# Two TensorE allowances in an order account, and two more adds of exp by DMA, in a fused attention and expert kernel

## The chip, the cores and the metric

The kernel runs on one core of a Trainium2 chip. The metric is the device time of one execution in microseconds (us), as a median over several executions. Almost all executions of one build lie within 0.3% of its median, the widest within 0.4%. Every profiled run of this study was of the fast state. A ratio is the mean time of one kernel's fast runs over the mean of the other's fast runs of the same rounds, so it is not quite the ratio of the medians that are quoted beside it. All verdicts use ratios to the kernel before; 0.01 is 35 us.

PE is TensorE's matmul, PEld its weight load, DVE VectorE, ACT ScalarE, POOL GpSimd, SP SyncE. "Attention" is here the time from the first exp of layer 0's attention to the last, "the tail" the time from there to the start of the experts' gated products, "experts" the rest.

## The reference, cut to what matters

The input is 8 images of 256 channels and 32 x 32 points, all in fp32.

```python
# layer 0: 8 heads of 32 channels; keys and values are the maps pooled by 1, 2, 3 and 6 and convolved
attn = softmax(einsum('bhqd,bhkd->bhqk', q_g, k) * SCALE)      # q: 1024 points, k: NK pooled points
out_att = einsum('bhqk,bhkd->bhqd', attn, v)
...                                                            # mixing by a global token, projection
x = x + layer0(groupnorm(x))
# layer 1 on the tokens of each image, then 8 experts with soft gates
t = t + attention(layernorm(t))                                # x @ Wq, Wk, Wv, softmax over 1024 tokens
t = t + experts(layernorm(t))
```

## The kernel before: the parts that matter here

The kernel is one program whose order is made while it is built. The main loop walks through the 384 steps of layer 0's attention (8 images, 2 groups of four heads, 2 halves of the points, 12 chunks of keys). Everything else, layer 1 too, is a thread of small pieces, which an "order account" slips in between.

```python
for i in range(len(steps) + 1):
    ...
        pts[i] = scores(b, c, sl, kc)          # 4 tiled matmuls into sc (one buffer), exp by ScalarE into pt
        f.step()                               # threads of the other engines may go ahead
    ...
        values(b1, c1, kc1, pts[i - 1], pv)    # 4 tiled matmuls from pt
        if kc1 % 2:                            # odd chunk: added to the even one, by DMA
            add(kc1, pts.pop(i - 1), pts[i - 2])
            pairs.append(pts.pop(i - 2))
    ...
        f.step(PACE)                           # threads may now use PACE us of TensorE

def scores(b, c, sl, kc):
    ...
    pt = T(work, [P, 4, 512], "pt", bufs=6)    # six buffers of 1 MB for exp
    f.act.activation(pt[:w], t[:w], AF.Exp, scale=SCALE0)

def add(kc, pt, into):                         # accumulating DMA, issued by GpSimd
    f.pool.dma_start(out=into..., in_=pt..., accum_op=ALU.add)

def sums(n, pairs):                            # the sum of exp of one unit (12 steps, 6 pairs)
    for i in range(1, NKC // 2):
        yield until(lambda: len(pairs) > i)
        for j in range(0, 4, 2):               # pairs 1 to 5 onto pair 0, by VectorE
            s = pairs[0][:, j : j + 2, :]
            yield ve(s, pairs[i])
            f.ve.tensor_tensor(s, s, pairs[i][:, j : j + 2, :], ALU.add)
```

The account holds an estimated clock for each engine. A thread's next matmul is put in if its data would be there in time, and if the thread's use of TensorE in this step is within the allowance `PACE` (or TensorE would wait for the exp anyway):

```python
def runnable(self, need):
    ...
        return (not self.closed and (self.credit > 0 or pe < until - 0.5)
                and at + MARGIN <= until and slot <= until)

def resume(self, thread):
    pe = self.now["PE"]
    thread[1] = next(thread[0], None)
    ...
    self.credit -= self.now["PE"] - pe
```

The account also assumes a landing time for DMAs that GpSimd issues, `LANDING = 9.5` us. It decides only which pieces are taken to be ready; the hardware waits for the real landing.

## Time and profile before

| | before |
|---|---|
| time, median of 3 (6 with later rounds) | 3497.31 us (3496.12) |
| profiled execution's span | 3505.2 us |
| attention / tail / experts | 1993.9 / 304.3 / 1100.2 us |
| PE idle in attention / tail | 191 / 27.0 us |
| ScalarE's wait for a pt buffer held by a DMA add | 56.9 us in 17 waits |
| DMA engines' busy share in attention | 0.54 to 0.56 |

PE is the busiest engine in every stage, so an engine's idle time counts only where PE in turn waits for that engine. "PE sc <- ACT pt" is such a line: the scores have one buffer, and PE may not overwrite it until exp has read it. If exp itself stands in front of a pt buffer that a DMA still reads, PE's wait is a DMA's doing although the line names ScalarE. The lines themselves are in the prediction.

### The profile page before, as it was taken

The numbers are of one execution on the slowest core, as the hardware profiler recorded it, in microseconds if no ns is written. First come the engines' busy times: TensorE is split into PE (matmuls) and PEld (weight loads), VectorE is DVE, ScalarE is ACT, GpSimd is POOL, SyncE is SP. The second block draws the span as 40 slices with busy tenths as digits, with TensorE's granted clock in tenths as the row PEclk, the third lists the DMA queues.
The fourth block names the chain that finished last, engine by engine and source line by source line (L and its number), as shares of the span: only waits on it lengthen the run. The fifth ranks groups of instructions, "written<-read, shape, count | busy, mean of one in ns | idle before, by whom it ended". The sixth has DMA issues, their size and how long they took to land.

```text
span 3505.2 us, 39918 instructions
## 1 busy us (share of the span) xinstructions
PE 3237.3 (92%) x15276; PEld 1790.8 (51%) x15276; DVE 2278.6 (65%) x3922; ACT 1676.3 (48%) x2195; POOL 489.1 (14%) x616
## 2 busy tenths in 40 slices
PE   7787899899989989989999997998999999999998
PEld 3322244344424434433544354745777777777776
DVE  6686888778878787685554443314776656666665
ACT  3565766556566565555564542332223333333332
POOL 2122122131131221321121110004000000000000
PEclk9798999999999999999999999999999999999999
DMA  1356655645655564554555556223440000000000
GB/s 47 75 107 152 134 127 111 144 108 111 148 105 110 134 136 109 119 124 111 112 125 136 128 105 219 79 79 107 150 150 19 19 18 24 31 18 19 19 12 20
DMA packets 103880, 333.28 MB, mean 95 GB/s; under 512 B 12848, under 2 KB 38200, under 8 KB 80448
## 3 DMA queue, kind: packets, MB, share of 16 engines
q0 software_dynamic: 24576, 172.51, 25.1%
q1 hardware_dynamic: 75744, 156.16, 13.0%
q8 instruction: 122, 2.00, 0.2%
q10 hardware_dynamic: 3360, 1.97, 0.2%
q14 instruction: 78, 0.64, 0.1%
HBM read 96.23 MB, written 61.87 MB: 45 GB/s over the span
## 4 chain that ended last, share of the span: by engine, by line
PE 53%; DMA 3%; DVE 3%; ACT 2%; issue 1%; POOL 0%; SPq 0%; DVEq 0%; ACTq 0%; POOLq 0%
PE bank L667 24%; PE y L667 11%; PE sm L667 9%; PE sc L667 3%; PE sx L667 3%; PE pv L667 3%; ACT pt L667 2%; DMA pt<-pt 1%; DMA t<-xr 1%; DVE acc L667 1%; DVE rec L667 1%; DMA t<-t 0%; DMA hn<-hn 0%; DMA xr<-in_x_dram 0%; DVE t L667 0%
## 5 line engine op out<-in xcount | busy, mean ns | idle before, releaser
L667 ACT ACTIVATE pt<-sc 128x2048 f32<-128x2048 f32 (+1 forms) x384 | 720.5, 1876 | 358.5 <-PE sc L667 263.0
L667 PE MATMUL sc<-q,kn 32*128 32x512 f32 (+1 forms) x3072 | 460.8, 671 | 134.1 <-ACT pt L667 132.7
L667 DVE SCALAR_TENSOR_TENSOR acc<-p,vec,acc 128x225 f32<-128x225 f32 (+7 forms) x928 | 521.1, 568 | 34.0 <-ACT acc L667 9.3
L667 PE MATMUL bank<-h,w2e 128*128 128x512 f32 x1024 | 481.2, 596 | 0.0
L667 ACT ACTIVATE h<-bank,bnvec 128x512 f32<-128x512 f32 x298 | 229.7, 771 | 480.0 <-PE bank L667 480.0
L667 DVE TENSOR_TENSOR pt<-pt,pt 128x1024 f32<-128x1024 f32 x320 | 383.8, 1242 | 104.7 <-DMA pt<-pt 100.0
L667 PE MATMUL pv<-pt,vt 128*32 128x512 f32 (+1 forms) x3072 | 429.5, 632 | 2.1 <-ACT att L667 2.1
L667 ACT ACTIVATE h<-c,bnvec 128x512 f32<-128x512 f32 x214 | 162.5, 807 | 322.9 <-DVE c L667 322.9
L667 POOL DMA_DIRECT2D pt<-pt x192 | 169.2, 881 | 994.7 <-ACT pt L667 872.4
L667 PEld LDWEIGHTS sc<-q,kn 32*128 32x128 f32 (+1 forms) x3072 | 119.8, 184 | 339.6 <-ACT pt L667 232.4
L667 DVE TENSOR_TENSOR c<-p1c,bank 128x512 f32<-128x512 f32 x107 | 73.6, 688 | 316.9 <-PE bank L667 316.9
L667 PEld LDWEIGHTS bank<-h,w2e 128*128 128x128 f32 x1024 | 194.8, 191 | 151.7 <-issue 139.9
L667 PEld LDWEIGHTS pv<-pt,vt 128*32 128x32 f32 (+1 forms) x3072 | 61.3, 109 | 315.3 <-issue 296.5
L667 POOL TENSOR_TENSOR rstd<-rstd,mhalf 128x4 f32<-128x4 f32 (+2 forms) x88 | 108.8, 1237 | 735.4 <-DVE rstd L667 602.0
L667 DVE TENSOR_TENSOR h<-h,gates 128x1024 f32<-128x1024 f32 x128 | 156.9, 1226 | 71.5 <-DMA h<-h 64.4
L667 PE MATMUL bank<-hn,w1e 128*128 128x256 f32 (+1 forms) x596 | 189.9, 447 | 10.5 <-DMA w2e<-in_w_dram 10.5
L667 PE MATMUL y<-t,s3e 128*128 128x256 f32 x768 | 187.5, 380 | 0.0
L667 PE MATMUL sm<-y,t 128*128 128x256 f32 x736 | 173.2, 383 | 0.0
L667 ACT ACTIVATE p<-sm 128x512 f32<-128x512 f32 (+1 forms) x151 | 88.2, 584 | 169.6 <-PE sm L667 143.5
L667 PEld LDWEIGHTS bank<-hn,w1e 128*128 128x128 f32 x596 | 114.0, 192 | 100.4 <-issue 92.7
L667 DVE RECIPROCAL rec<-rec 128x512 f32<-128x512 f32 x32 | 107.3, 3352 | 89.1 <-ACT rec L667 89.0
L667 PE MATMUL bank<-t,s1e 128*128 128x256 f32 x642 | 156.1, 379 | 2.9 <-DVE t L667 2.9
(291 smaller groups left out, 4679.2 us busy)
## 6 DMA issues: line engine op xcount, KB each, us to landing
pt<-pt POOLq DMA_DIRECT2D x160, 1024.0 KB, 7.4
h<-h SPq DMA_DIRECT2D x72, 512.0 KB, 4.0
xi<-in_x_dram SPq DMA_DIRECT2D x16, 512.0 KB, 7.2
t<-t SPq DMA_DIRECT2D x8, 1024.0 KB, 5.8
res<-t SPq DMA_DIRECT2D x32, 256.0 KB, 6.0
t<-o SPq DMA_DIRECT2D x32, 256.0 KB, 2.8
hn<-o SPq DMA_DIRECT2D x32, 256.0 KB, 5.6
hn<-hn SPq DMA_DIRECT2D x16, 512.0 KB, 5.3
```

Source lines behind the costliest of these rows:

```text
L667: ins = fn(*args, **kwargs)
```

## The change

The intent: give VectorE less to do, by moving two of its five adds of exp per unit to DMA, which does six already and then has eight of the eleven; give layer 0's own small work (ranks under 5) and layer 1 (the rest) separate allowances, so that layer 1 neither crowds it out nor runs dry; and let the account know what a change of the array's tiling costs. Cut to its core:

```diff
-PACE = 3.2
-CAP = 1.5
+FILLER = 5
+PACE = 4.0
+PACE1 = 2.0
+CAP = (1.5, 1.5)
+BY_DMA = (2, 4)
...
-            return c / 4 + 0.05 if ins[0].shape[0] <= DH or ins[0].shape[1] <= DH else c
+            return c if self.tiling(ins) is None else c / 4
...
+            tiling = None if op == "transpose" else self.tiling(srcs)
+            if tiling != self.tiled:
+                cost += {None: 0.09, "rows": 0.2, "columns": 0.13}[tiling]
+                self.tiled = tiling
...
-                and (self.credit > 0 or pe < until - 0.5)
+                and (self.credit[rank >= FILLER] > 0 or pe < until - 0.5)
...
-        self.credit -= self.now["PE"] - pe
+        self.credit[thread[2] >= FILLER] -= self.now["PE"] - pe
...
             for i in range(1, NKC // 2):
                 yield until(lambda: len(pairs) > i)
+                if i in BY_DMA:
+                    yield pool(pairs[0], pairs[i])
+                    add(0, pairs[i], pairs[0])
+                    continue
...
-                res = T(l1, [P, 2, C], "res")
+                yield until(lambda: scaled[0] >= i - 1)
+                res = T(l1, [P, 2, C], "res", bufs=2)
...
-                yield from scale_tokens(o, C)
-                f.sp.dma_start(hn[b][:, :, q], o)
...
+                f.spawn(norm(b, q, res), 5)      # layer 1's norm is a thread of its own
...
-                f.step(PACE)
+                f.step((PACE, PACE1))
```

More of the change, by code (lines that the diff above doesn't have):

```diff
@@ L686, in __init__ @@
         self.also = {}
-        self.credit, self.port = 0.0, 0.0
+        self.tiled = None
+        self.credit, self.port = [0.0, 0.0], 0.0
     def tile(self, pool, shape, tag, bufs=1):
@@ L734, in cost, with tiling @@
         return 0.15 + 0.00107 * n
+    @staticmethod
+    def tiling(ins):
+        rows, columns = ins[0].shape[0], ins[0].shape[-1]
+        return "columns" if columns <= DH and rows > 8 else "rows" if rows == DH else None
     def note(self, engine, op, ins, args, kwargs):
@@ L758, in note @@
         cost = self.cost(engine, op, out, srcs)
+        if engine == "PE":
+            tiling = None if op == "transpose" else self.tiling(srcs)
+            if tiling != self.tiled:
+                cost += {None: 0.09, "rows": 0.2, "columns": 0.13}[tiling]
+                self.tiled = tiling
         wide = [a for a in srcs if a.space != PSUM and a.free_size() > 4]
@@ L803, in spawn, with runnable @@
         return thread
-    def runnable(self, need):
+    def runnable(self, need, rank=0):
         engine, tiles, tag = need
@@ L836, in step @@
         if pace is not None:
-            self.credit = min(self.credit + pace, CAP * pace)
+            for i in range(2):
+                self.credit[i] = min(self.credit[i] + pace[i], CAP[i] * pace[i])
         while True:
-            thread = next((t for t in self.threads if self.runnable(t[1])), None)
+            thread = next((t for t in self.threads if self.runnable(t[1], t[2])), None)
             if thread is None:
@@ L846, in finish @@
         while not done():
-            self.credit, self.closed = 1.0, False
+            self.credit, self.closed = [1.0, 1.0], False
             thread = next((t for t in self.threads if t[1][0] is None and self.runnable(t[1])), None)
@@ L910, in attention @@
         ident, grp = kit.ident, con[:, K_GRP : K_GRP + P]
-        heads = T(l1, [P, P + DH], "o")
+        heads = T(l1, [P, P + DH], "res", bufs=2)
         nc.scalar.dma_start(heads, consts[:, K_HEAD:K_SEL])
@@ L1300, in pool_levels @@
             for i, (a, e) in enumerate(ends):
-                yield ve(xi)
+                yield ve(xi, t5)
                 f.ve.tensor_reduce(t5[:, :, :, i], img[:, :, :, a:e], AX.X, ALU.add)
@@ L1644, in outputs, with norm @@
                 yield ve(ps, rec)
-                o = T(l1, [P, 2, C], "o")
-                f.ve.tensor_tensor(
-                    o, ps.rearrange("p (m q) -> p m q", m=2), rec[:, None, :].to_broadcast([P, 2, C]), ALU.mult
-                )
+                m2 = ps.rearrange("p (m q) -> p m q", m=2)
+                f.ve.tensor_tensor(m2, m2, rec[:, None, :].to_broadcast([P, 2, C]), ALU.mult)
                 for m in range(2):
-                    f.ve.scalar_tensor_tensor(o[:, m, :], o[:, m, :], gb[:, m : m + 1], res[:, m, :], ALU.add, ALU.add)
-                f.sp.dma_start(t2[b][:, :, q], o)
-                yield from scale_tokens(o, C)
-                f.sp.dma_start(hn[b][:, :, q], o)
-                written[0] += 1
-                ended[0] = written[0] // 4
+                    f.ve.scalar_tensor_tensor(res[:, m, :], m2[:, m, :], gb[:, m : m + 1], res[:, m, :], ALU.add, ALU.add)
+                f.sp.dma_start(t2[b][:, :, q], res)
+                f.spawn(norm(b, q, res), 5)
+        scaled = [0]
+        def norm(b, q, o):
+            yield from scale_tokens(o, C)
+            f.sp.dma_start(hn[b][:, :, q], o)
+            scaled[0] += 1
+            written[0] += 1
+            ended[0] = written[0] // 4
         def centred(cm, src, width, dst):
@@ L1741, in weights1 @@
             for e in range(NE):
-                we = T(l1, [P, 2, C], "res")
+                we = T(l1, [P, 2, C], "res", bufs=2)
                 f.sp.dma_start(we, w1_d[:, e])
                 yield act(we)
-                wc = T(l1, [P, 2, C], "o")
+                wc = T(l1, [P, 2, C], "res", bufs=2)
                 yield from centred(cm, we, C, wc)
@@ L2116, in experts @@
             n1 += 1
-            f.step(PACE2)
+            f.step((PACE2, PACE2))
             if n1 > 1:
@@ L2121, in experts @@
                 n2 += 1
-                f.step(PACE2)
+                f.step((PACE2, PACE2))
         f.finish(lambda: gated)
```

## The prediction

> **What bounds the kernel now.** I began with the page's busy times by engine and its forty slices, then cut the span into stages with the view of busy time by stretch.
>
> ```profile
> PE 3237.3 (92%) x15276; PEld 1790.8 (51%) x15276; DVE 2278.6 (65%) x3922; ACT 1676.3 (48%) x2195; POOL 489.1 (14%) x616
> ...
> PE   7787899899989989989999997998999999999998
> ...
> PEclk9798999999999999999999999999999999999999
> ```
>
> TensorE (PE) is busy for 92% and nothing else comes near. The stages (columns: stretch and length, then busy time and instruction count of each engine, granted clock, DMA share, GB/s):
>
> ```profile
> 100.00:460.00 360.00, 289.00 (x1620) 104.73 (x1620) 270.40 (x536) 223.98 (x263) 71.71 (x83) 0.89 0.55 122
> 460.00:1740.00 1280.00, 1176.57 (x6480) 536.04 (x6477) 990.31 (x1767) 771.73 (x948) 280.99 (x336) 0.97 0.54 121
> 1740.00:2100.00 360.00, 342.64 (x1977) 169.92 (x1976) 177.88 (x258) 190.50 (x202) 52.55 (x60) 0.98 0.56 123
> 2100.00:2405.00 305.00, 278.02 (x867) 155.63 (x865) 78.64 (x138) 98.83 (x155) 23.56 (x39) 0.96 0.34 120
> 2405.00:3506.00 1101.00, 1083.51 (x4156) 790.58 (x4156) 698.48 (x1082) 354.31 (x553) 26.71 (x42) 0.99 0.13 45
> ```
>
> Attention of layer 0 fills 100 to 2100 us (384 steps, so 5.2 us each), with layer 1 threaded between its matmuls; 2100 to 2405 is a tail, in which layer 1 of the last image must end while the experts' first products fill TensorE; the rest is experts. The change does not touch the last stretch, where PE is 98% busy at a clock of 0.99. In attention PE is idle for 2000 - (289.0 + 1176.6 + 342.6) = 192 us. The clock not granted there is worth 0.11 x 360 + 0.03 x 1280 + 0.02 x 360 = 85 us more. About 277 us is thus all that a better order could win in attention, 27 us of idle in the tail besides.
>
> What PE waits for, from the view of waits and the groups of attention (100 to 2100 us):
>
> ```profile
> PE sc L667 <- ACT pt L667: 132.7, 96, 7.6
> ...
> DVE pt L667 <- DMA pt<-pt: 100.0, 41, 12.5
> ...
> ACT pt L667 <- DMA pt<-pt: 56.9, 17, 7.5
> ...
> ACT p L667 <- DVE acc L667: 33.7, 13, 6.2
> ...
> PE sm L667 <- DVE xr L667: 23.7, 6, 5.9
> ```
>
> Of PE's 192 us, 133 us is scores (sc, one buffer) waiting for the exp (pt) of the step before. I went through these 96 waits in the trace and asked what ScalarE had been held by: for 50 us exp had followed its scores at once, so PE simply had too little other work; for 43 us exp had waited for a buffer of pt that a DMA add still held; for about 15 us ScalarE stood in front of a map copy whose buffer VectorE was still convolving; the rest is small. VectorE itself is busy for 1439 of 2000 us.
>
> ```profile
> L667 ACT ACTIVATE pt<-sc 128x2048 f32<-128x2048 f32 (+1 forms) x384 | 720.5, 1876 | 358.5 <-PE sc L667 263.0 <-DMA pt<-pt 56.9 <-issue 12.6
> ...
> L667 DVE TENSOR_TENSOR pt<-pt,pt 128x1024 f32<-128x1024 f32 x318 | 381.5, 1242 | 104.7 <-DMA pt<-pt 100.0 <-ACT p L667 4.7
> ...
> L667 POOL DMA_DIRECT2D pt<-pt x191 | 168.4, 882 | 984.6 <-ACT pt L667 862.4 <-PE sm L667 48.1 <-DVE acc L667 37.0
> ```
>
> **What the Trainium skill says.** "TensorE: Matmul & The Clock Gate", Part 1: the array's clock is halved after an idle window of about 3.4 us. The trace agrees: its clock records are 1.0 or 0.5 only, and the stretch with most idle (71 of 360 us) has 0.89. So idle costs more than itself. "TensorEngine Tiling (Array Packing)", Key Properties: changing the tiling mode drains the array. In the timeline a score group of four tiled matmuls starts 1.07 us before the value group, and that 1.00 us before the next full matmul, where the two passes of one 512-column product take 0.86 us (0.43 each in the experts' stage): 0.21 and 0.14 us a change. "DMA: Bandwidth & Descriptors", Anatomy of one DMA: 2.0 us plus bytes at 436 GB/s, which is 4.4 us for 1 MB; the accumulating pt<-pt takes 7.4 us (median, the page's list of DMA issues), so the trace's figure is used. "VectorE: DVE Perf Modes", Mode 1x: one fp32 result a cycle at 0.96 GHz, 1.07 us for 1024; the trace has 1.242.
>
> **The change part by part.**
>
> *Two adds of exp by DMA.* A unit (12 steps) makes six pairs of exp; the odd one is added to the even one by DMA, and pairs 1 to 5 are added to pair 0 by VectorE, in two halves. Pairs 2 and 4 now go by DMA. Over 32 units VectorE loses 2 x 2 x 32 = 128 adds x 1.242 = 159 us, which takes its load in attention from 72% to 64%. As it is not the bound, only what it holds up counts: at most the 15 us above, and about 10 us of work that the order can place earlier in the first 460 us, where VectorE is 75% busy and PE lacks work. I take -25 us.
> Against it: 64 more DMA adds on 192. Queue 0 took 43.9% of 16 engines for 191 of them in 2000 us, or 4.6 us each; 64 more add 294 us, or 15 points, so the DMA engines go from 55% to 70%. The even buffer of such a pair is now freed after two landings one behind the other (2 x 8.3 us with the issue) in place of one and an add (8.3 + 2.5 us), and all landings become slower. From the built programs' order, exp takes a buffer again mostly three or four steps (16 to 21 us) after its last use is issued, and for the odd tiles the share of four falls from 158 of 186 to 110. I let PE's 43 us of buffer waits grow by 40%: +17 us. The second add also stands in GpSimd's in-order queue behind the landing of the first, in front of small rstd and diag work: +3 us.
>
> *Two allowances.* Layer 0 may use 4.0 us a step and layer 1 2.0, in place of 3.2 for both. The work stays the same, but its place changes. In the built order the matmuls of layer 1 after the last scores rise from 233 to 330. Most are 256 columns wide at 0.445 us, so some 41 us leaves attention and enters the tail: no gain, except that the tail's idle may swallow some, -5 us. Within attention it becomes more even: with the measured intervals, the filling that steps lack to reach 1.1 us (a step without any took 3.18 us in the timeline, scores and values are 2.07 of it) falls from 86 to 74 us in total. That sum answers to 50 us measured, so 12 x 50 / 86 = -7 us. The experts' plain first and second halves before the gates are 84 and 80 matmuls in both orders.
>
> *The account's tiling.* The old account took 0.266 us for each of four tiled matmuls, 1.06 us a group; the new one 0.216 x 4 + 0.2 = 1.07 and 0.216 x 4 + 0.13 = 1.00. Almost nothing moves because of it: 0.
>
> *Layer 1's norm as its own thread, and two res buffers.* It takes a wait out of each quarter's chain; the tail is 91% full, so I count it in the -5 us.
>
> Sum of idle: -25 + 17 + 3 - 5 - 7 = -17 us. Each us of idle in attention comes with 85 / 192 = 0.44 us of lost clock, so -17 x 1.44 = -24 us, and 3473 us. I choose 3460, 13 us lower, because the allowances look fitted on the chip and would hardly have been kept for nothing; this part is judgement.
>
> **The rivals.** (1) *Buffers of pt become the wait.* If ScalarE's wait for DMA doubles from 57 us, PE loses 43 x 1.44 = 62 us instead of 17 x 1.44 = 24, and the time is about 3500: the relief is eaten. For it: landings of 9 to 11 us stand in the chain of waits already. Against it: three to four steps of slack are over 15 us. (2) *VectorE was the hidden bound of the first 460 us.* If 5 us a unit there and the clock come back, and similar in the middle, idle falls by some 60 us and the time is about 3400. For it: 87% busy in single 100 us stretches and a clock of 0.81 to 0.93. Against it: PE's waits hardly name VectorE. (3) *The work put off hurts the tail*: 41 us more there and attention not shorter, because steps with less filling wait for exp: about 3500. Against it: late steps keep 138 / 71 = 1.9 us of filling on average, over the 1.1 that hides exp.
>
> **Range and chances.** The order is made anew throughout, which alone may move tens of us either way. The two ends are near the rivals' 3400 and 3500: 3400 to 3508. Over 2% faster is under 3427, which needs rival 2: 0.19. Over 2% slower is above 3567, beyond all that I can add up: 0.03.
>
> **What would show it.** Right: 192 adds of pt on VectorE and 256 of DMA; VectorE's busy time near 2120 us; DMA share in attention near 0.70; ScalarE's wait for pt<-pt at 70 to 85 us; attention ending some 50 to 80 us earlier and the tail about 35 us longer; the experts' stage as before, near 1100 us. Wrong: DMA waits above 110 us (rival 1), or a PE idle in attention below 140 us with a clock over 0.95 in the first 460 us (rival 2), or attention as long as before (rival 3).

## The result

The changed kernel takes 3499.69 us (median of 6 runs, 3495.59 to 3510.82) against 3496.12 us (6 runs, 3487.26 to 3504.50) for the one before: ratio 1.0017, 95% interval 0.9995 to 1.0039. Nothing was gained; 37 us were forecast. The two profiled executions differ the other way (3505.2 and 3493.8 us), because before's profiled run lies at the top of its kind's scatter and after's at the bottom, so they are compared stage by stage and not by their sums.

The page of the changed kernel, busy times and slices:

```profile
PE 3230.7 (92%) x15276; PEld 1786.3 (51%) x15276; DVE 2142.1 (61%) x3794; ACT 1674.1 (48%) x2195; POOL 553.9 (16%) x680
...
PE   7777789979989989999999999999999999999998
...
PEclk9888899999989999999999999999999999999999
```

VectorE lost 2278.6 - 2142.1 = 136.5 us, most of the 159 us forecast. TensorE's slices look as before: the work left VectorE, and PE did not notice. The view of busy time by stretch, cut at the changed kernel's own stages (columns: stretch and length, then busy time and instruction count of PE, PEld, DVE, ACT, POOL, granted clock, DMA share, GB/s):

```profile
100.00:460.00 360.00, 281.41 (x1532) 102.77 (x1532) 249.02 (x518) 217.46 (x262) 79.07 (x88) 0.89 0.67 147
460.00:1740.00 1280.00, 1173.77 (x6488) 529.28 (x6484) 888.57 (x1659) 769.00 (x939) 315.42 (x380) 0.96 0.71 154
1740.00:2071.00 331.00, 312.99 (x1875) 142.26 (x1874) 137.71 (x204) 188.89 (x188) 61.97 (x71) 0.99 0.83 174
2071.00:2395.00 324.00, 311.94 (x1049) 187.47 (x1047) 95.86 (x171) 107.56 (x177) 24.88 (x31) 0.98 0.36 121
2395.00:3494.00 1099.00, 1084.01 (x4156) 790.98 (x4156) 700.35 (x1083) 354.37 (x553) 36.78 (x55) 0.99 0.13 45
```

Attention ends at 2070.9 instead of 2100.7 us, 30 us sooner; the tail is 324.4 instead of 304.3 us, 20 us longer, although PE's idle time there fell from 27.0 to 12.1 us. PE's busy time in the tail rose from 278.0 to 311.9 us: 34 us of work was put off, more than the whole 30 us by which attention ended sooner. PE's idle in attention is 1971 - (281.4 + 1173.8 + 313.0) = 203 us, more than before's 192 in 2000, and the clock of the first 460 us is the same 0.89. The DMA share rose from 0.55 to 0.67 and beyond.

What waits, from the view of waits and the groups of attention:

```profile
PE sc L670 <- ACT pt L670: 143.9, 89, 10.5
POOL pt L670 <- DMA pt<-pt: 129.9, 22, 11.1
...
ACT pt L670 <- DMA pt<-pt: 122.2, 44, 9.1
...
DVE pt L670 <- DMA pt<-pt: 102.4, 25, 13.4
```

```profile
L670 ACT ACTIVATE pt<-sc 128x2048 f32<-128x2048 f32 (+1 forms) x384 | 720.6, 1877 | 400.1 <-PE sc L670 241.7 <-DMA pt<-pt 122.2 <-issue 12.8
...
L670 DVE TENSOR_TENSOR pt<-pt,pt 128x1024 f32<-128x1024 f32 x192 | 233.3, 1256 | 103.8 <-DMA pt<-pt 102.4 <-issue 1.2
L670 POOL DMA_DIRECT2D pt<-pt x256 | 225.4, 908 | 1031.1 <-ACT pt L670 680.6 <-DMA pt<-pt 129.9 <-DVE acc L670 96.7
```

ScalarE's wait for pt buffers doubled, from 56.9 us in 17 waits to 122.2 us in 44. That is over the 110 us that the prediction had set as the mark of rival 1. GpSimd, which never waited for a landing before, now does for 129.9 us: its second add stands behind the first's landing. This agrees with the Trainium skill, "DMA: Bandwidth & Descriptors", Anatomy of one DMA, which has the semaphore wait of a DMA happen at the issuing engine ahead of the transfer.

### The profile page after: what moved, and what is told of

It reads as the page before. It is cut to its first block, busy times and chain, and to the rows that moved or that the text cites. A ratio compares the mean times of both kernels' runs of the same rounds, so it can differ in the third digit from the quotient of the medians.

```text
span 3493.8 us, 39923 instructions
## 1 busy us (share of the span) xinstructions
PE 3230.7 (92%) x15276; PEld 1786.3 (51%) x15276; DVE 2142.1 (61%) x3794; ACT 1674.1 (48%) x2195; POOL 553.9 (16%) x680
## 4 chain that ended last, share of the span: by engine, by line
PE 58%; DMA 4%; DVE 3%; ACT 2%; issue 1%; POOL 0%; SPq 0%; ACTq 0%; DVEq 0%; POOLq 0%
PE bank L670 24%; PE y L670 11%; PE sm L670 11%; PE sc L670 5%; PE sx L670 4%; PE pv L670 4%; DVE acc L670 1%; ACT pt L670 1%; DMA pt<-pt 1%; DMA t<-xr 1%; DMA hn<-pool 1%; DMA xr<-in_x_dram 1%; DMA t<-t 1%; DVE rec L670 0%; DVE t L670 0%
## 5 line engine op out<-in xcount | busy, mean ns | idle before, releaser
L670 POOL DMA_DIRECT2D pt<-pt x256 | 225.4, 908 | 1031.1 <-ACT pt L670 680.6
L670 DVE TENSOR_TENSOR pt<-pt,pt 128x1024 f32<-128x1024 f32 x192 | 233.3, 1256 | 103.8 <-DMA pt<-pt 102.4
L670 PE MATMUL sm<-y,t 128*128 128x256 f32 x768 | 183.1, 385 | 1.8 <-DVE st L670 0.9
L670 PEld LDWEIGHTS sm<-y,t 128*128 128x128 f32 x768 | 141.3, 190 | 56.2 <-issue 27.9
L670 PE MATMUL sm<-p,v 128*128 128x256 f32 x704 | 165.1, 384 | 2.0 <-ACT pool L670 1.6
```

The source lines that it names most:

```text
L670: ins = fn(*args, **kwargs)
```

## The experiments

The theory after the result: the allowances, the account and the norm thread win, and the two DMA adds lose about as much, through pt buffers held longer (theory H) and through the bytes that slow all landings (theory T). The rivals: the allowances won nothing (R1), VectorE's relief was worth much but was eaten (R2), and, after twelve runs, the size of each part is the luck of one order (R3). The first twelve experiments have one order each; how far an order alone moves the time is measured only by the last six, and the sizes given before are to be read with that. In all, 18 kernels ran; every one but e11 (on purpose) gave the right result. A test with one more or one fewer pt buffer was not possible: with five the order can't be completed, and seven need 157 KB of a partition where 149.3 KB are free.

### Parts undone or done alone

**e1_no_dma**: the changed kernel without its two DMA adds.

```diff
-BY_DMA = (2, 4)
+BY_DMA = ()
```

> The changed kernel with all five pair adds of a unit back on VectorE; allowances, account and norm thread kept. Theory A (buffers): the two adds by DMA double ScalarE's wait for pt<-pt (57 us before, 122 after) and eat what the rest wins; without them that wait falls back to 50 to 70 us and the time to some 3475 us, 0.5 to 0.9% under the kernel before. Theory B (VectorE): the adds by DMA do help, and the loss is in the allowances or the account; then this kernel is slower than the changed one, 3510 to 3530 us. Theory C (every part is worth nothing beyond the scatter of a new order): within 10 us of the kernel before, although the wait for pt<-pt falls back.

3427.69 us (3421.53 to 3432.28), ratio 0.979 (0.9768 to 0.9812): 73 us faster than before, and faster than both kernels of this case. Its stretches of attention and its waits:

```profile
100.00:460.00 360.00, 292.46 (x1656) 106.38 (x1656) 285.11 (x548) 225.43 (x269) 73.09 (x84) 0.92 0.56 124
460.00:1740.00 1280.00, 1206.00 (x6806) 551.72 (x6806) 1005.96 (x1813) 804.90 (x986) 287.39 (x350) 0.98 0.57 127
1740.00:1993.00 253.00, 245.53 (x1429) 108.55 (x1429) 123.03 (x149) 142.20 (x134) 37.77 (x41) 0.98 0.63 134
```

```profile
PE sc L670 <- ACT pt L670: 109.0, 84, 7.9
...
ACT pt L670 <- DMA pt<-pt: 50.3, 17, 6.6
```

PE idles 1893 - (292.5 + 1206.0 + 245.5) = 149 us in attention, 54 us less than the changed kernel, and attention is 2071 - 1993 = 78 us shorter. The share 78 / 54 = 1.44 is the prediction's factor for the lost clock, found again in this pair. VectorE is busier here than in the changed kernel in each of the first two stretches (285 against 249 us in the first), and PE idles less: in this pair it is not VectorE's load that PE waits for. Whether the relief was worth something that the adds ate (R2) is asked by e11.

**e2_dma_only**: the kernel before with the DMA adds alone.

```diff
+BY_DMA = (2, 4)
...
+                if i in BY_DMA:
+                    yield pool(pairs[0], pairs[i])
+                    add(0, pairs[i], pairs[0])
+                    continue
```

> The kernel before with pairs 2 and 4 added by DMA, and nothing else. Theory A: ScalarE's wait for pt<-pt at 100 to 130 us, VectorE about 135 us less busy, time 10 to 25 us longer than before. Theory B: 10 to 25 us shorter. Theory C: within 10 us either way.

3593.18 us, ratio 1.0263 (1.0241 to 1.0286): 92 us slower than before. From the view of waits over its attention:

```profile
POOL pt L668 <- DMA pt<-pt: 177.0, 27, 14.8
PE sc L668 <- ACT pt L668: 169.7, 100, 7.1
ACT pt L668 <- DMA pt<-pt: 141.2, 39, 7.3
```

Alone, the part of the change that was to relieve the kernel costs it 92 us, and PE's wait for exp goes from 132.7 to 169.7 us.

**e3_dma_all**: the changed kernel with all five adds by DMA.

```diff
-BY_DMA = (2, 4)
+BY_DMA = (1, 2, 3, 4, 5)
```

> The changed kernel with all five pair adds of a unit by DMA: 352 adds by DMA, none by VectorE; the dose is 2.5 times that of the change. Theory A: ScalarE's wait for pt<-pt at 200 us or more, attention 30 to 80 us longer than in the changed kernel, total 3530 to 3580 us. Theory B: VectorE near 1910 us busy, and the time at or under the changed kernel's. Theory C: DMA waits rise, but PE fills them with other work, and the time stays within 15 us of 3500.

3740.38 us, ratio 1.0682 (1.0658 to 1.0706). From its waits and its DMA issues:

```profile
ACT pt L670 <- DMA pt<-pt: 390.9, 132, 9.5
...
PE sc L670 <- ACT pt L670: 247.1, 131, 7.6
```

```profile
pt<-pt POOLq DMA_DIRECT2D x320, 1024.0 KB, 9.4
```

Here one sees the cost run away: the median landing of the adds of 1 MB goes from 7.3 us (e1, 192 adds in all) over 7.6 (the changed kernel, 256) to 9.4 (352), and ScalarE's wait from 50 over 122 to 391 us.

**e4_one_allowance**: the changed kernel with one allowance of 3.2 us for all threads.

```diff
-PACE = 4.0
-PACE1 = 2.0
+PACE = 3.2
+PACE1 = 3.2
...
-                and (self.credit[rank >= FILLER] > 0 or pe < until - 0.5)
+                and (self.credit[0] > 0 or pe < until - 0.5)
...
-        self.credit[thread[2] >= FILLER] -= self.now["PE"] - pe
+        self.credit[0] -= self.now["PE"] - pe
```

> The changed kernel with one allowance of 3.2 us a step for all fillers, as before; adds by DMA, account and norm thread kept. Theory A: 3490 to 3510 us, since the DMA waits stay; fewer matmuls of layer 1 after the last scores than the changed kernel's 330, a shorter tail and a longer attention. Theory B: the two allowances were the loss, so 3470 to 3480 us here. Theory C: within 10 us of the kernel before.

3563.51 us, ratio 1.0176 (1.0154 to 1.0198). This speaks against R1 for this form of the kernel: with the DMA adds in, the two allowances are worth 56 to 64 us in these two orders (3563.51 less the changed kernel's 3499.69, or 0.0159 of the ratio).

### Which side of the DMA adds costs

**e5_traffic_only**: e1 with 64 DMAs of 1 MB that hold no pt buffer: from the input to spare memory, at the places where the DMA adds stood. VectorE still does the adds.

```diff
+                if i in (2, 4):
+                    yield pool(pairs[0], pairs[i])
+                    spare = kit.spare[turns[0] % 4]
+                    turns[0] += 1
+                    f.pool.dma_start(spare, x[turns[0] % nb].rearrange("(p k) n -> p (k n)", p=P))
                 for j in range(0, 4, 2):
```

> The kernel of e1_no_dma, all pair adds on VectorE, with 64 further DMAs of 1 MB from GpSimd's queue at the places where pairs 2 and 4 would be added by DMA; they copy the input to a spare place in DRAM, so they load the DMA engines and GpSimd's queue but hold no exp buffer. Against e1 (3428 us): theory of the hold (the two landings one behind the other keep the even buffers 27 us in place of 21) says 3428 to 3445 us, as only the odd landings get some 0.8 us slower; theory of the traffic (engines 70% busy, GpSimd's queue) says 3475 to 3510 us.

3487.76 us, ratio 0.9966 (0.9954 to 0.9978): 60 us slower than e1, without a pt buffer held for the new transfers. They run from DRAM to DRAM, which the adds do not.

**e6_late_adds**: e1 with VectorE's adds of pairs 2 and 4 held back until the next pair stands, which holds the buffers and moves no bytes.

```diff
+                if i in (2, 4):
+                    yield until(lambda: len(pairs) > i + 1)
                 for j in range(0, 4, 2):
```

> The kernel of e1_no_dma, with VectorE's adds of pairs 2 and 4 held back until the next pair stands: the buffers are held longer, without a single DMA more. Theory of the hold: the mean hold of even buffers rises by 3 us or more from 20.7 us, ScalarE's wait for pt rises from 50 us to 90 us or more, and the time to 3460 to 3510 us. Theory of the traffic: within 15 us of e1's 3428 us.

3467.57 us, ratio 0.9915 (0.99 to 0.9929), 40 us slower than e1. It looked like a proof of theory H, but it isn't one: ScalarE's wait for pt rose only from 50.3 to 58.1 us, although the even buffers of pairs 2 and 4 were held for 24.9 us on average in place of 20.6 (from the start of exp to the end of the last add), and all even buffers for 22.4 in place of 20.7, less than the 3 us more that I had expected. The edit also makes a new order, on which more below. I count it as inconclusive.

**e7_no_dma_one_allowance**: e1 with e4's edit.

> The kernel of e1_no_dma with the one allowance of 3.2 us a step for all fillers, so that of the whole change only the account of tilings and the norm thread are left. If the two allowances are what wins the 73 us of e1 against the kernel before: 3480 to 3500 us. If account or norm thread win it: 3430 to 3450 us. From the pair after and e4, which differ in the same way by 64 us, I expect the first.

3452.63 us, ratio 0.9865 (0.9846 to 0.9884). Without the DMA adds the allowances are worth 25 us, not 64 (one order of each).

**e8_no_dma_old_account**: e1 with the old cost of tiled matmuls.

```diff
-            return c if self.tiling(ins) is None else c / 4
+            return c / 4 + 0.05 if ins[0].shape[0] <= DH or ins[0].shape[1] <= DH else c
...
-            if tiling != self.tiled:
+            if False:
```

> The kernel of e1_no_dma with the old cost of tiled matmuls in the account (a quarter plus 0.05 us, no cost for a change of tiling). My prediction gave this part 0 us: then within 12 us of e1's 3428 us. If knowing the changes of tiling is worth something, 3440 to 3480 us.

3445.81 us, ratio 0.9848 (0.9832 to 0.9864): 18 us slower than e1.

### A control, the norm thread, the relief alone, and a tuning

**e9_tiny_dmas**: e5 with its 64 DMAs cut to eight columns. The built programs of e5 and e9 have the same order on every engine, so the bytes are the only difference.

```diff
-                    f.pool.dma_start(spare, x[turns[0] % nb].rearrange("(p k) n -> p (k n)", p=P))
+                    f.pool.dma_start(spare[:, :8], x[turns[0] % nb].rearrange("(p k) n -> p (k n)", p=P)[:, :8])
```

> e5_traffic_only with its 64 spare DMAs shrunk from 1 MB to eight columns of 128 partitions (4 KB); by the built programs the order of instructions on every engine is the same as in e5, so only the bytes differ. If the bytes of the added DMAs are what e5 lost (60 us against e1_no_dma), this takes about 3430 us, within 12 us of e1's 3427.7, and its landings of pt<-pt go back from 7.9 to about 7.3 us. If instead e5 lost by its new order of work or by the places its DMAs took in GpSimd's queue, this stays near e5's 3488.

3452.30 us, ratio 0.9865 (0.985 to 0.9881). Neither answer alone: the bytes cost 3487.76 - 3452.30 = 35 us, and the other 25 us of e5's loss came with 64 transfers of 4 KB, that is, with a new order of everything. The pair shows how bytes cost. Waits of attention of e9, then of e5:

```profile
PE sc L670 <- ACT pt L670: 111.0, 89, 11.5
...
DVE pt L670 <- DMA pt<-pt: 68.3, 30, 7.1
...
ACT pt L670 <- DMA pt<-pt: 48.6, 13, 11.9
...
DVE xr L670 <- DMA xr<-in_x_dram: 36.8, 12, 7.1
```

```profile
PE sc L670 <- ACT pt L670: 110.6, 90, 7.4
...
DVE pt L670 <- DMA pt<-pt: 101.9, 39, 6.9
...
DVE xr L670 <- DMA xr<-in_x_dram: 63.7, 13, 8.8
...
ACT pt L670 <- DMA pt<-pt: 49.9, 14, 8.4
...
PE sm L670 <- DVE xr L670: 21.2, 7, 4.7
```

PE's wait for exp and ScalarE's wait for pt are the same in both. What grew is VectorE's wait for landings, of the DMA adds (68 to 102 us) and of the input blocks xr (37 to 64 us), and through the latter PE's wait for VectorE to empty an sm bank: 21.2 us in e5, 4.6 us in e9. The traffic hurts where nobody had looked, around the projection. With the same order the transfers can be compared one by one: the loads of xr themselves land hardly later (4.6 us on average in e5, 4.3 in e9), but the stores of the block that was in the buffer before them (t<-xr) take 5.2 in place of 4.0 us, and SyncE waits 103.7 in place of 74.1 us for them before it issues. Added up over attention, PE's waits outside the scores go from 57 to 82 us, which is 25 of the 26 us by which its idle time grows. What this pair doesn't show is what the adds' own traffic costs: it is of another kind, and the DMA share here is 0.66 in attention (0.57 in e9) against 0.72 in the changed kernel.

**e10_no_dma_norm_inline**: e1 with layer 1's norm back in its quarter's chain.

```diff
-                f.spawn(norm(b, q, res), 5)
+                yield from norm(b, q, res)
```

> e1_no_dma with layer 1's norm put back into its quarter's chain (the two res buffers stay). The gain of e1 over the kernel before is 73 us, of which single allowances undo 25 (e7) and the old account 18 (e8); if the parts add up, the norm thread is the remaining 30, and this takes about 3458 us. If the parts interact, or the order's own scatter of tens of us is what these small differences show, it takes 3425 to 3445 instead. The prediction's value for the thread (a share of 5 us) would put it at about 3430.

3459.93 us, ratio 0.9887 (0.9871 to 0.9902), 32 us slower than e1 and what adding up had asked for. That the sum fitted proved nothing, as the last runs show.

**e11_relief_only**: e1 with VectorE's adds of pairs 2 and 4 cut to 16 of 512 columns and done by nothing else. The result is wrong on purpose.

```diff
+                    w = 16 if i in (2, 4) else 512
-                    s = pairs[0][:, j : j + 2, :]
+                    s = pairs[0][:, j : j + 2, :w]
```

> e1_no_dma with VectorE's adds of pairs 2 and 4 shortened from 2 x 512 to 2 x 16 columns and not done by anything else; its result is wrong on purpose. VectorE loses some 130 us of busy time and no DMA is added, so this is the relief alone. The prediction's value for it is -25 x 1.44 = -36 us: about 3392. If VectorE is a hidden bound of attention (rival 2), more than that: 3370 or less. If VectorE holds nothing up once the allowances are in, the gain is that the even buffers come free sooner only, or none: 3415 to 3430.

3407.32 us, ratio 0.9744 (0.9729 to 0.9759). VectorE's busy time falls from 2281.5 to 2159.5 us, and the time by 20 us (0.0046 in ratio, 16 us). That is less than the 36 on record, but the order is a new one here too (TensorE's differs from e1's from the 500th matmul on), and e1's was a lucky one, as the last runs show: against the mean of e1's three orders this run is 53 us faster. So the relief is not sized, and R2, a larger relief eaten, is weakened and not excluded.

**e12_pace1_25**: e1 with layer 1's allowance 2.5 instead of 2.0, a try at a still faster version.

```diff
-PACE1 = 2.0
+PACE1 = 2.5
```

> e1_no_dma with layer 1's allowance at 2.5 us a step in place of 2.0, a try at a faster version. Layer 1 would end earlier, so the tail should be 5 to 10 us shorter; attention gets it back if its steps keep over 1.1 us of filling: 3415 to 3440, most likely the same as e1 within 10 us. If the narrower allowance is what keeps filling even, 3440 to 3455.

3495.16 us, ratio 0.9997 (0.9987 to 1.0006). This missed every value I had expected: 68 us lost with one constant moved, though ScalarE's wait for pt was 47.3 us, less than e1's. It made me doubt the sizes of all parts.

### How far an order scatters

The last six runs rebuild three kernels with a change that means nothing: the account's assumed landing time moved by 0.1 or 0.2 us. The program's work is the same (15264 to 15282 matmuls in the six), but its order differs almost throughout.

```diff
-LANDING = 9.5
+LANDING = 9.3     # e13, e14, e15; 9.7 in e16 and e18, 9.6 in e17
```

**e13_before_landing_93** and **e17_before_landing_96** (the kernel before; with 9.7 it fails the check before the chip):

> The kernel before with the account's assumed landing time 9.3 us in place of 9.5: the same work in another order. If orders scatter by 10 to 15 us, this takes 3480 to 3510 us. If the scatter is as large as the parts measured so far, it may lie anywhere from 3440 to 3560.

> The kernel before with the account's assumed landing time 9.6 us in place of 9.5, a third order of it. 3480 to 3510 us if orders scatter by 10 to 15 us; wider if they scatter as much as the parts.

**e14_after_landing_93** and **e18_after_landing_97** (the changed kernel):

> The changed kernel with 9.3 us for 9.5. Scatter of 10 to 15 us: 3485 to 3515. If the changed kernel was lucky or unlucky, it moves by 30 us or more; a value under 3440 would mean that the DMA adds cost nothing and the first order was unlucky.

> The changed kernel with 9.7 us for 9.5, a third order of it. 3485 to 3515 us if orders scatter by 10 to 15 us. If the mean of its three orders comes within 15 us of the mean of the three without DMA adds, the cost of the DMA adds is not shown.

**e15_no_dma_landing_93** and **e16_no_dma_landing_97** (e1):

> e1_no_dma with 9.3 us for 9.5. If e1's gain of 73 us is the parts and not luck: 3415 to 3445. If e1 was a lucky order: 3450 to 3490.

> e1_no_dma with 9.7 us for 9.5, a third order: 3415 to 3445 if the gain is the parts, 3450 to 3490 if e1 was lucky.

| kernel | 9.5 us | 9.3 us | 9.6 or 9.7 us | mean ratio |
|---|---|---|---|---|
| before | 1 | 0.9978 (3490.77) | 0.9907 (3462.41) | 0.9962 |
| changed | 1.0017 (3499.69) | 1.0031 (3510.19) | 1.0112 (3534.51) | 1.0053 |
| changed without DMA adds | 0.979 (3427.69) | 0.9919 (3471.69) | 0.9975 (3490.75) | 0.9895 |

Every ratio's own interval is within 0.0025 of it, so these are real differences between orders. Orders that mean the same differ by 33 to 65 us among three. e1 was the luckiest of its three. That settles what may be said:

- *The DMA adds cost time: shown.* The three changed orders (1.0017 and up) are all above the three without DMA adds (0.9975 and down); the means are 0.0158 apart, 55 us. Over all kernels with the whole work and no added transfers or delays, the ten without the adds (the six of the table's first and last rows, e7, e8, e10, e12) are at 0.979 to 1, the five with two of them (the table's middle row, e2, e4) at 1.0017 to 1.0263.
- *The rest of the change wins something: not shown.* Before's three orders have a mean of 0.9962, e1's three 0.9895: 23 us, but the groups overlap. The single worths of the account (e8, 18 us) and of the norm thread (e10, 32 us), as well as e6's 40 us, lie inside the 65 us by which e1's own orders differ.
- *ScalarE's wait for pt goes with the DMA adds and not with the order.* In the ten orders without them it is 37 to 75 us, in the five with two of them 98 to 141 us. One line of each extreme, e16 and e4:

```profile
ACT pt L670 <- DMA pt<-pt: 74.9, 22, 8.0
```

```profile
ACT pt L670 <- DMA pt<-pt: 97.8, 32, 6.2
```

- *The two allowances empty the tail's gaps: shown for the tail.* PE's idle time in the tail is 25 to 45 us in the six kernels of these fifteen with one allowance of 3.2 (24.8, 27.0, 27.0, 30.6, 41.8, 45.0), and 12 to 24 us in the eight with 4.0 and 2.0. For the whole time: one allowance 1.0263 and 1.0176 against 1.0017 to 1.0112 with the adds, so the groups are apart; 0.9865 to 1 against 0.979 to 0.9975 without the adds, so they overlap.

e1_no_dma remains the build that beats both kernels, 3427.69 us over five runs whose range is 11 us. Its order is fixed once built, so its gain is real; but some 37 us of the 73 (its 0.979 against its group's 0.9895) is the luck of that order, and a small edit elsewhere may lose it.

## Why the prediction was wrong

The time was forecast at 3460 and came to 3499.69 us. The range of 3400 to 3508 held it, and "same" had the most weight, but the gain of 37 us was not there. By its steps:

**The step that failed: the balance of the two adds by DMA, "-25" against "+17" and "+3".** On record it was a small gain, -5 us of idle, or -5 x 1.44 = -7 us. Measured over three orders each (the changed kernel and the one without the adds), it is 36 us more idle of PE in attention (means 205 and 169) and a loss of 55 us (mean ratios 1.0053 and 0.9895). PE's waits, added up from the traces by what ended them, say where: +19 us behind the adds' hold of pt, +26 us outside the scores, -9 us in the other waits at the scores. So the hold was sized about right; what failed is a relief of 25 us that on balance no wait shows, and slower landings that got no number. Term by term:

- *The relief, -25, or -36 with the clock.* The count was right (192 adds left, VectorE at 2142.1 us against "near 2120"). The worth is not settled: e11 is 20 us faster than e1, but one order. With the adds PE's other waits at the scores are 9 us shorter and all its remaining waits longer, so if more relief is there, the next terms hide it.
- *The buffer wait, "I let PE's 43 us of buffer waits grow by 40%: +17 us".* PE's waits for an exp whose own wait ended with a landing of pt<-pt are 42.6 us in the kernel before and 59.7 in the changed one, +17. Over three orders each they are 59.3 us on average with the adds and 40.5 without, +19. This term came out; between orders it scatters widely (23.5 to 48.4 us in the ten orders without the adds, 56.4 to 85.2 in the five with them). ScalarE's own wait, forecast at 70 to 85 us, came to 122.2. The argument that held this down ("three to four steps of slack are over 15 us") had missed how far the hold grows: the even buffers of pairs 2 and 4 are held for 27.1 us on average from the start of exp to their release in the changed kernel, against 20.6 in e1, and those that VectorE still adds for 23.6 us, against 20.8; I put the latter down to pair 0, which is busy with the DMA's add.
- *"and all landings become slower".* This stood in the prediction with no number, and is the largest term found. PE's waits outside the scores, for banks and data of layer 1 and of layer 0's other work, are 57, 76 and 84 us in the three changed orders and 38, 46 and 55 in e1's three, +26 us on average. In the pair with equal order (e5, e9), further traffic alone makes the same waits 25 us longer and the time 35 us, as much as the whole forecast gain. That the adds' 26 us come from their traffic in the same way is argued from this, not shown; the longer stand of GpSimd's queue is another candidate. The DMA share itself was foreseen well (0.70; 0.67, 0.71 and 0.83 in the three stretches): a share of 0.7 was seen and not priced.
- *GpSimd's queue, +3.* GpSimd waits 129.9 us for landings, but most odd adds are not delayed: from the end of exp to their issue the trace has a median of 0.3 us in the kernels with and without the added adds. What the queue costs behind them the trace doesn't resolve.

**The allowances, "-7" and "-5".** The move of layer 1 was right: 34 us of work went to the tail (41 forecast), the tail grew by 20 us (35 forecast), and attention ended 30 us sooner (50 to 80 forecast). The tail's idle fell by 15 us in this pair where 5 were taken. PE's waits where exp followed its scores within 0.5 us fell from 51.4 to 37.4 us, for which 7 were taken. Both were somewhat low in this pair. With the adds in, the allowances bring about 58 us (mean 1.0220 of e2 and e4 against 1.0053, of which the account and the norm thread may have a part); without them, 19 us or nothing (0.9938 of before's three and e7 against 0.9884 of e1, e8, e10, e15, e16, overlapping). Why they help more beside the DMA adds I have not settled.

**The account's tiling, "0", and the norm thread.** Single runs say 18 and 32 us, both within the scatter of orders. Zero can't be refuted.

**The factor 1.44.** It is 1.44 between e1 and the changed kernel (78 us of attention for 54 us of idle), 1.6 between the means of their three orders (57 for 36), and 1.2 between e9 and e5 (30 for 26): right in its middle, and no constant.

**The judgement, "13 us lower, because the allowances look fitted on the chip".** A tuner can fit the luck of an order as well. e12 shows how much one constant can move: 0.5 us more of allowance, and 68 us are gone.

**The scatter of orders.** "The order is made anew throughout, which alone may move tens of us either way" is the truest sentence of the prediction; the groups of three spread by 33 to 65 us. A forecast gain of 37 us was less than that, so this pair alone could show neither the gain nor its absence. What the groups say is that the changed kernel is, if anything, the slower: 1.0053 against 0.9962.

**The rivals.** Rival 1 came true in its sign, ScalarE's wait for DMA (57 to 122 us), but not in its price: PE was to lose 43 us more to the hold and lost 17 in this pair, so that its time, "about 3500", was met by other terms. Rival 2 fell in this pair: PE's idle in attention was not below 140 us, and the clock of the first stretch stayed at 0.89. Rival 3 is half there: attention did shorten, but by no more than the work that went into the tail; the steps with less filling did not make it longer. The experts' stage was untouched, 1098.5 us against 1100.2.

## What to carry to other kernels

An add moved from a busy engine to DMA is not free just because that engine gets less to do: price the longer hold of its buffers, and the other landings on which the new bytes fall, from a control in which only the bytes differ, and are of the same kind. Where a scheduler builds the order, measure its scatter first, with changes that mean nothing; a difference smaller than that belongs to no part of the change until several orders of each form are apart. And when a bundled change shows no gain, undo its parts one by one: here one part hid a build that measures 2% faster than both, about half of it by the luck of its order.

## What the Trainium skill lacked or had wrong

- "DMA: Bandwidth & Descriptors", Anatomy of one DMA: the fit of 2.0 us plus bytes at 436 GB/s gives 4.4 us for 1 MB. Accumulating DMAs of 1 MB within the core's memory land after a median of 7.2 to 7.4 us with 192 adds in the program, 7.6 to 8.0 us with 256 and 9.4 us with 352. The page has no figure for accumulating ones, so this is a gap and not an error of the fit.
- The same page has no figure for what further traffic costs the transfers beside it at a DMA share well under 1: with the share at 0.66 in place of 0.57 (e5 and e9, equal order), the stores t<-xr took 5.2 us on average in place of 4.0, and VectorE's wait for the loads xr that follow them went from 36.8 to 63.7 us.
- "TensorEngine Tiling (Array Packing)", Key Properties: it says that a change of mode drains the array and gives no time. In the timeline of the kernel before, four matmuls in row tiles take 0.21 us and four in column tiles 0.14 us more than the two passes of a full matmul; the prediction and the account put this down to the change.
